# A post-norm attention layer on one core: first keys in float32 from the raw loads, maxima spread through DRAM, and own places for the last unit

## The chip, the core and the metric

The kernel runs on one core of a Trainium2 chip. The core has TensorE (matrix products, in the profile PE, its weight loads PEld), VectorE (DVE), ScalarE (ACT), GpSimd (POOL) and SyncE (SP, which here only issues DMAs). The metric is the device time of one execution in microseconds (us); three runs of the kernel before gave 1235.85 us in the median (1235.78 to 1237.4). A difference is given against that median.

## The reference, cut to what matters

Eight sequences of 1024 tokens, 512 features, 16 heads of 32. The attention is linear: queries and keys go through random features, and the keys' features are summed with the values first.

```python
def feature_map(x, orf):                       # orf: 128 x 32
    proj = x @ orf.T / d_k ** 0.25
    norm = jnp.sum(x * x, -1, keepdims=True) / (2.0 * math.sqrt(d_k))
    return (jnp.exp(proj - norm) + 1e-6) / math.sqrt(m)
q = feature_map(split(x @ Wq.T + bq), orf)
k = feature_map(split(x @ Wk.T + bk), orf)
v = split(x @ Wv.T + bv)
buf = concatenate([einsum('nlm,nld->nmd', k, v), sum(k, 1)[..., None]], -1)
out = einsum('nlm,nmd->nld', q, buf)
attn = merge(out[..., :-1] / out[..., -1:]) @ Wo.T + bo
x = layernorm(x + attn)
x = layernorm(x + x @ (ternary(W) * mean(abs(W))).T)
```

Outputs are float32.

## The kernel before, in words

**Blocks and splits.** The 8192 tokens are worked in 16 blocks of 512, two to a sequence. The products with Wk, Wv, Wq and Wo run in float16: each operand is scaled by a power of two, worked out from its largest magnitude, and split into a high and a low half (`high` on ScalarE, `low` on VectorE); a projection is the sum of three products, high times high, low times high, high times low, twelve instructions of 128x512 for each 128 outputs. In the profile these are k_ps, v_ps, q_ps and o_ps (L353, L366), and xh, xl, wh, wl are the halves.

**The largest magnitude.** `Largest` takes the maximum along each partition on VectorE (amax, then acol, one column of 128). To have the maximum of all partitions in every partition, TensorE turns the column into a row (`turn`, amt, L202), VectorE takes the row's maximum (`across`, arow, L207), and TensorE spreads it with a product with ones (`spread`, ams, L211). `scale` then makes the powers of two on VectorE in six or seven one-column steps. This is done once for each of the four weights and for each of the 16 blocks of x.

**A block's way.** Keys: projection, clamp and split on VectorE and ScalarE, a trip through DRAM that stacks the parts head by head (ds, st; the squared norms go by dn), features (kf_ps, L626), exponentials on ScalarE (e), and the sums over tokens (kvt_ps on TensorE, esum and vsum on GpSimd). After the second block of a sequence `close` finishes the sums (vs_ps, ks_ps, kv_tp, kv) and `out_scale` works out the scale of the attention's output. Queries go the same way (qf_ps, L765) and then meet the sums (num_ps and den, L784); the denominators go through DRAM to be inverted and spread (dd, r, dr, rb), the quotient (num, L852) is split (oh, ol), projected (o_ps), added to the residual y, normalized, turned (x_tp), multiplied by the ternary weight (f_ps), normalized again and stored.

**The order.** Nothing is scheduled by the tool: the class `Order` sorts every step by a written place, in us, and by what it needs. `pe` and `gen` steps are TensorE's; `after` puts a step so much later than a TensorE step ends, `at` puts it at a place. Each engine and SP's DMA queue then work strictly in that order. A unit is one block's stretch: while the keys and values of block t are made, the queries of earlier blocks are applied and still earlier ones finished. `units` holds the first units' places; the later ones are 74 apart. `E` is the place where the last block's unit ends.

**The head.** The raw loads of w_k (SP) and of x's block 0 (ScalarE's queue) come in four pieces each; VectorE takes their maxima, TensorE spreads them, both are split, and the first key projection can begin. w_v, w_q and w_o are loaded into places that other tiles use later (`STAGING`): w_q and w_o both into the tile rb, which w_k occupies first.

**Buffers that the steps touch.** The pool pj has six PSUM buffers for all products but two accumulators; y has five row tiles; xraw, rb and esum have one each.

Of the kernel before, what the change touches and what calls it, by code (L numbers as in the profile page):

```python
# [9 lines left out]
F32 = mybir.dt.float32  # L10
F16 = mybir.dt.float16
AF = mybir.ActivationFunctionType
# [41 lines left out]
STAGING = {"k": "rb", "v": "esum", "q": "rb", "o": "rb"}  # L54
# [4 lines left out]
class Order:  # L59
# [7 lines left out]
    DRAW = 2.5  # L67
# [63 lines left out]
def tile_postln_layer(  # L131
# [49 lines left out]
    class Largest:  # L181
# [33 lines left out]

        def steps(self, place, gap=3.0, needs=()):

            step = order.pe(place, 0.15, self.turn, needs=needs)
            gate = order.after(step, 0.2, self.across)
            return order.pe(place + gap, 0.15, self.spread, needs=[gate])  # L220
# [27 lines left out]
    class W:  # L248
# [6 lines left out]
        def load(self):  # L255
            self.raw = block(STAGING[self.which], f"wraw_{self.which}")
            nc.sync.dma_start(self.raw, self.src.rearrange("(k p) o -> p k o", p=P))

        def measure(self):
            self.largest.whole(self.raw)  # L260
            self.largest.close()
# [13 lines left out]
        def high(self, kt):  # L275
            nc.scalar.activation(self.h[:, kt, :], self.raw[:, kt, :], AF.Copy, scale=wup[:, self.c])

        def low(self, kt):
            c, raw = self.c, self.raw[:, kt, :]
# [13 lines left out]
    class X:  # L293
# [22 lines left out]
        def unscale(self, which):  # L316

            for w in which:
                d = small([P, 1], f"down_{w}_{self.t}", 24)
                nc.vector.tensor_mul(d, xdown[:, self.c], wdn[:, weights[w].c])  # L320
# [52 lines left out]
    ws = {which: W(src, which) for which, src in (("k", wkT), ("v", wvT), ("q", wqT), ("o", woT))}  # L373
    for w in ws.values():
        w.tiles()
    x0, w0 = X(0), ws["k"]
    w0.raw, x0.raw = block(STAGING["k"], "wraw_k"), block("xraw", "xraw_0")
    for kt in range(KT):
        nc.sync.dma_start(w0.raw[:, kt, :], wkT[kt * P : (kt + 1) * P, :])
        nc.scalar.dma_start(x0.raw[:, kt, :], xT[kt * P : (kt + 1) * P, 0:TB])  # L380
        w0.largest.piece(kt, w0.raw[:, kt, :])
        x0.largest.piece(kt, x0.raw[:, kt, :])


    class Bias:


        def __init__(self, src, which):
# [3 lines left out]
            nc.scalar.dma_start(self.b, src)  # L392
# [8 lines left out]
    biases = {"k": bk, "q": bq}  # L401
    bv_sb = ctile([P, D], F32, "bv_sb")
# [76 lines left out]
    class Stacked:  # L479
# [45 lines left out]
        def project(self, i, places):  # L525
            step = gen(places, 0.87, self.proj(i), needs=self.ready)
            w = self.which
            clamp = after(step, {"k": 0.02, "q": 0.02}[w], self.clamp, i)
            high = after(step, {"k": 1.89, "q": 1.13}[w], self.high, i, needs=[clamp])
            rest = after(step, {"k": 5.33, "q": 3.44}[w], self.remainder, i, needs=[high])  # L530
            s1 = after(step, {"k": 8.5, "q": 2.45}[w], self.spill, i, 1, needs=[high])
            low = after(step, {"k": 7.53, "q": 6.16}[w], self.low, i, needs=[rest])
            s0 = after(step, {"k": 11.3, "q": 6.97}[w], self.spill, i, 0, needs=[low, s1])
# [26 lines left out]
        def norms(self, place):  # L560
            w = self.which
            step = pe(place, 1.0, self.norm, needs=self.sq_gates, tiled=True)
            last = after(step, {"k": 4.37, "q": 0.02}[w], self.norm_high)
            last = after(step, {"k": 2.22, "q": 3.06}[w], self.norm_rest, needs=[last])
            last = after(step, {"k": 2.48, "q": 6.0}[w], self.norm_low, needs=[last])
            last = after(step, {"k": 6.55, "q": 3.88}[w], self.norm_store, needs=[last])
# [21 lines left out]
    class KBlock(Stacked):  # L588
# [27 lines left out]
        def values(self, tt, places, sums):  # L616
# [3 lines left out]
            self.sum_gates.append(after(step, 2.64, self.v_sum, tt, sums, needs=[bias, *self.sum_gates[-1:]]))  # L620
# [24 lines left out]
        def feature(self, i, tt, place, sums):  # L645
# [3 lines left out]
            self.sum_gates.append(after(step, 0.02, self.e_sum, i, tt, sums, needs=[exp]))  # L649
# [88 lines left out]
        def close(self, places, sums):  # L738

            step = pe(places[0], 1.0, self.v_total, sums, needs=[*self.sum_gates, self.last_kv])  # L740
            g0 = after(step, 3.32, self.close_kv, sums)
            step = pe(places[1], 1.2, self.k_total, sums, needs=[g0, *self.sum_gates], tiled=True)
            g1 = after(step, 1.64, self.close_sums)
            step = pe(places[2], 0.9, self.turn, 0, needs=[g0])
            g0 = after(step, 0.84, self.keep, 0)
            step = pe(places[2] + 2.87, 0.9, self.turn, 1, needs=[g0, g1])
            kv_ready[self.b] = after(step, 0.72, self.keep, 1)
            at(places[2] + 5.87, self.out_scale, needs=[*self.ready, self.bv_ready])
# [4 lines left out]
    class QBlock(Stacked):  # L753
# [80 lines left out]
        def attend(self, i, place):  # L834
            step = pe(place, 1.9, self.products, i, needs=[kv_ready[self.b], *(self.gates[HPT * i + j] for j in range(HPT))], tiled=True)
            self.num_gates.append(after(step, 1.66, self.numerator, i))
            if i == KT - 1:
                last = after(step, 0.58, self.denominator)
                for delay, fn in (
                    (1.4, self.denominator_store),  # L840
                    (6.99, self.recip_load),
                    (4.48, self.recip),
                    (7.84, self.recip_store),
                ):
                    last = after(step, delay, fn, needs=[last])
                for j in range(HPT):
                    gap = 0.76 if self.t < NBLK - 2 else 0.0
                    last = after(step, 5.61 + gap * j, self.recip_spread, j, needs=[last])
# [15 lines left out]
        def divide(self, i, place):  # L864
            num = at(place, self.quotient, i, needs=[self.num_gates[i], self.spread])
            high = at(place + 0.72, self.out_high, i, needs=[num])
# [25 lines left out]
        def layernorm(self, step, last, tt, name):  # L892

            w = name[0]
            last = after(step, {"a": 1.5, "f": 1.61}[w], self.moments, tt, name, needs=[last])
            last = after(step, {"a": 0.02, "f": 6.55}[w], self.power, name, needs=[last])
            last = after(step, {"a": 4.16, "f": 1.31}[w], self.shift, name, needs=[last])
            last = after(step, {"a": 5.74, "f": 7.76}[w], self.apply, tt, name, needs=[last])
# [291 lines left out]
```

## Time and profile before

| | |
|---|---|
| median of 3 runs | 1235.85 us |
| the profiled execution's own time | 1237.1 us |
| its span | 1235.3 us |
| mean granted TensorE clock | 0.991 |
| TensorE busy | 1187.5 us, 96% |
| VectorE, ScalarE, GpSimd busy | 854.7, 832.3, 525.2 us |
| DMA | 169 MB, 137 GB/s in the mean |
| first product of block 0's keys | 14.64 us |
| last product | 1225.6 us |

A row of a timeline gives the start in us, the length in us, the engine (SPq is SP's DMA queue), the line, the operation, what it writes and reads, shapes and types, how many instructions were merged (a float32 product counts as two), and in brackets the idle time of the engine just before and what ended it. A row of the waits gives who waited for what, the total us, how many times, and the longest.

### The profile page before, as it was taken

How to read it: one execution, taken by the hardware profiler on the slowest of the kernel's cores; microseconds unless marked ns; L12 is line 12 of the kernel's file. 1: busy time of each engine (PE TensorE's matmuls, PEld its weight loads, DVE VectorE, ACT ScalarE, POOL GpSimd, SP SyncE). 2: the span in 40 equal slices, each digit the busy share in tenths (PEclk: the TensorE clock that was granted, in tenths of full speed). 3: DMA queues.
4: the chain of work that ended last, by engine and by line, in shares of the span. 5: the costliest groups of instructions: out<-in, count | busy, mean ns of one | idle time of the engine just before them, and what ended most of it. 6: DMA issues, size and time to landing. Idle time of an engine off the chain costs nothing.

```text
span 1235.3 us, 23801 instructions
## 1 busy us (share of the span) xinstructions
PE 1187.5 (96%) x8724; PEld 572.1 (46%) x8724; DVE 854.7 (69%) x1849; ACT 832.3 (67%) x1377; POOL 525.2 (43%) x485
## 2 busy tenths in 40 slices
PE   5899999999999999999999999999999999999987
PEld 2344454545545454454545445453544545454333
DVE  7775665776857756686766848577674876648387
ACT  3486678666766867668686667867686776756643
POOL 0148062724446153552627334372444515354222
PEclk9899999999999999999999999999999999999989
DMA  4445455363554536444453545546355453536421
GB/s 164 145 136 160 132 138 168 104 181 92 169 143 127 158 102 187 107 156 135 123 169 102 170 133 147 149 111 184 80 170 151 130 152 94 167 92 195 123 71 69
DMA packets 94821, 169.39 MB, mean 137 GB/s; under 512 B 14736, under 2 KB 48624, under 8 KB 92656
## 3 DMA queue, kind: packets, MB, share of 16 engines
q1 hardware_dynamic: 93296, 166.24, 46.8%
q8 instruction: 69, 1.13, 0.4%
q10 hardware_dynamic: 1408, 1.63, 0.4%
q14 instruction: 48, 0.39, 0.1%
HBM read 108.06 MB, written 59.77 MB: 136 GB/s over the span
## 4 chain that ended last, share of the span: by engine, by line
PE 81%; DVE 10%; ACT 2%; issue 1%; DMA 1%; POOL 0%; POOLq 0%; SPq 0%; ACTq 0%
PE o_ps L366 13%; PE v_ps L366 12%; PE q_ps L353 12%; PE k_ps L353 8%; PE f_ps L958 8%; PE num_ps L784 5%; PE kf_ps L626 5%; PE den L784 4%; PE kvt_ps L660 4%; PE qf_ps L765 4%; PE x_tp L935 2%; DVE num L852 1%; PE n_ps_k L541 1%; DVE ol L862 1%; DVE st_f L871 1%; DVE y L966 1%
## 5 line engine op out<-in xcount | busy, mean ns | idle before, releaser
L643 POOL TENSOR_TENSOR esum<-esum,e 128x512 f32<-128x512 f32 x192 | 248.0, 1294 | 136.8 <-ACT e L631 132.1
L631 ACT ACTIVATE e<-kf_ps 128x512 f32<-128x512 f32 x256 | 150.8, 597 | 124.1 <-PE kf_ps L626 112.1
L769 ACT ACTIVATE qf<-qf_ps 128x512 f32<-128x512 f32 x256 | 142.7, 610 | 44.4 <-PE qf_ps L765 44.4
L914 POOL TENSOR_TENSOR y<-y,bo_sb 128x512 f32<-128x512 f32 x64 | 82.8, 1296 | 110.4 <-DMA y<-in_x_dram 53.7
L880 POOL TENSOR_TENSOR rs_a<-ve_a,neg_half 128x1 f32<-128x1 f32 x64 | 35.8, 559 | 217.1 <-DVE ve_a L875 212.5
L626 PEld LDWEIGHTS <-st_k 98*128 98x128 f16 x1024 | 77.1, 97 | 63.5 <-issue 10.5
L626 PE MATMUL kf_ps<-of,st_k 98*128 98x128 f16 x1024 | 98.3, 219 | 2.5 <-DMA st_k<-dn_k 2.2
L602 DVE SCALAR_TENSOR_TENSOR v<-v_ps,down_v,bv_sb 128x512 f32<-128x512 f32 x64 | 47.7, 746 | 69.8 <-PE v_ps L366 69.6
L493 DVE TENSOR_SCALAR q_ps<-q_ps,top_q,bottom_q 128x512 f32<-128x512 f32 x64 | 52.2, 816 | 62.5 <-PE q_ps L353 62.4
L765 PE MATMUL qf_ps<-st_q,of 98*128 98x512 f16 x256 | 89.3, 382 | 2.2 <-ACT qf L769 1.1
L500 ACT ACTIVATE part_q<-q_ps,bq_sb,down_q 128x512 f16<-128x512 f32 x64 | 49.8, 778 | 56.8 <-DVE q_ps L493 51.2
L366 PEld LDWEIGHTS <-oh 128*128 128x128 f16 x512 | 49.3, 98 | 77.7 <-issue 12.7
L923 DVE SCALAR_TENSOR_TENSOR y<-o_ps,odown,y 128x512 f32<-128x512 f32 x64 | 48.0, 750 | 53.2 <-PE o_ps L366 47.2
L353 PEld LDWEIGHTS <-wh_k 128*128 128x128 f16 x512 | 48.9, 100 | 70.9 <-issue 18.6
L614 POOL TENSOR_TENSOR vsum<-vsum,v 128x512 f32<-128x512 f32 x48 | 62.7, 1306 | 37.7 <-DVE v L602 37.7
L880 POOL TENSOR_TENSOR rs_f<-ve_f,neg_half 128x1 f32<-128x1 f32 x64 | 49.3, 770 | 68.3 <-DVE ve_f L875 45.7
L643 POOL TENSOR_TENSOR esum<-e,e 128x512 f32<-128x512 f32 x32 | 41.1, 1285 | 87.1 <-ACT e L631 87.1
L500 ACT ACTIVATE part_k<-k_ps,bk_sb,down_k 128x512 f16<-128x512 f32 x64 | 50.1, 782 | 41.2 <-DVE k_ps L493 19.4
L366 PE MATMUL o_ps<-wh_o,oh 128*128 128x512 f16 x256 | 67.4, 384 | 8.7 <-DVE kv L723 5.2
L857 ACT CAST oh<-num 128x512 f16<-128x512 f32 x64 | 39.3, 616 | 47.2 <-DVE num L852 47.2
L353 PE MATMUL k_ps<-xh,wh_k 128*128 128x512 f16 x256 | 66.5, 384 | 4.1 <-ACT xh L335 4.0
L366 PEld LDWEIGHTS <-xh 128*128 128x128 f16 x512 | 46.3, 98 | 50.5 <-issue 7.9
(211 smaller groups left out, 2744.4 us busy)
## 6 DMA issues: line engine op xcount, KB each, us to landing
ds_k<-part_k SPq DMA_DIRECT2D x128, 128.0 KB
st_k<-ds_k SPq DMA_DIRECT2D x64, 256.0 KB
ds_q<-part_q SPq DMA_DIRECT2D x128, 128.0 KB
st_q<-ds_q SPq DMA_DIRECT2D x64, 256.0 KB
rb<-dr SPq DMA_DIRECT2D x64, 256.0 KB
y<-in_x_dram SPq DMA_DIRECT2D x64, 256.0 KB
out_dram<-y SPq DMA_DIRECT2D x64, 256.0 KB
xraw<-in_xT_dram SPq DMA_DIRECT2D x15, 1024.0 KB
```

The costliest lines, as they stand in the source:

```text
L353: nc.tensor.matmul(ps, a[:, kt, c], b[kt], start=(n == 0), stop=(n == 3 * KT - 1))
L366: nc.tensor.matmul(ps, a[kt][:, c], wt[:, kt, :], start=(n == 0), stop=(n == 3 * KT - 1))
L500: nc.scalar.activation(part[:, 1, :], self.ps[i], AF.Identity, bias=b, scale=down)
L626: nc.tensor.matmul(ps[:, j, :], self.st[i][0:NF, j, c], of, start=True, stop=True)
L631: nc.scalar.activation(e, self.eps[i, tt], AF.Exp, scale=EXP_SCALE)
L643: nc.gpsimd.tensor_tensor(es, before, self.es[i, tt].rearrange("p j m -> p (j m)"), op=ALU.add)
L765: nc.tensor.matmul(self.qps[n], of, self.st[i][0:NF, j, :], start=True, stop=True)
L769: nc.scalar.activation(e, self.qps[n], AF.Exp, scale=EXP_SCALE)
L784: nc.tensor.matmul(to[DK * j : DK * (j + 1), :], kvl[:, n, i * P + DK * j : i * P + DK * (j + 1)], self.qf[i, j], start=first, stop=last, ...
L880: nc.gpsimd.tensor_tensor(self.rs[name], self.ve[name], neg_half, op=ALU.pow)
L914: nc.gpsimd.tensor_tensor(y, y, bo_sb, op=ALU.add)
L958: nc.tensor.matmul(ps, a[:, kt, :], tern.w[:, kt, :], start=(n == 0), stop=(n == 2 * KT - 1))
```

## The change

Four things are changed together.

1. **Block 0's keys** are multiplied in float32 straight from the raw loads: `project_first` issues, for each of the four pieces, two pairs of 128x512 products. They need neither maxima nor halves; their scale (`down_k`) is a constant, and the clamp and all that follows are as before. w_k is still split, later, for the other blocks.
2. **The largest magnitudes** of w_k, w_q, w_o and of x's blocks 1 to 15 no longer go through TensorE: `store` writes the column of 128 to DRAM, `fetch` reads it back as a row into every partition, and `fold` takes the maximum of the row in each. Only x's block 0 and w_v keep the old way (`steps`).
3. **w_q** is loaded in four rows of its own into the y tiles (and so can be loaded from the start), w_o alone follows w_k in rb.
4. **The places**: nearly all written places and delays are new, the units' starts among them; the last unit (`t == NBLK - 1`) and unit `NBLK - 4` have places of their own, `out_scale` stands 22.06 after the closing's third place where it stood 5.87 after it, and `DRAW` is 2.35.

```diff
-STAGING = {"k": "rb", "v": "esum", "q": "rb", "o": "rb"}
+STAGING = {"k": "rb", "v": "esum", "q": "y", "o": "rb"}
...
-    DRAW = 2.5
+    DRAW = 2.35
...
+        def store(self):
+            self.dm = dram.tile([P, 1], F32, tag="dm", name=f"dm_{self.name}", bufs=4)
+            nc.sync.dma_start(self.dm, self.col)
+
+        def fetch(self):
+            self.every = sb.tile([P, P], F32, tag="every", name=f"every_{self.name}", bufs=2)
+            nc.sync.dma_start(self.every, self.dm.rearrange("p o -> o p").to_broadcast([P, P]))
+
+        def fold(self):
+            self.all = small([P, 1], f"aall_{self.name}", 24)
+            nc.vector.tensor_reduce(self.all, self.every, AX.X, ALU.max)
+
+        def passed(self, place, gaps, needs):
+            last = order.at(place + gaps[0], self.store, needs=needs)
+            last = order.at(place + gaps[1], self.fetch, needs=[last])
+            return order.at(place + gaps[2], self.fold, needs=[last])
...
-                nc.vector.tensor_mul(d, xdown[:, self.c], wdn[:, weights[w].c])
+                if self.t == 0 and w == "k":
+                    nc.vector.memset(d, QK_SCALE)
+                else:
+                    nc.vector.tensor_mul(d, xdown[:, self.c], wdn[:, weights[w].c])
...
-        w0.largest.piece(kt, w0.raw[:, kt, :])
         x0.largest.piece(kt, x0.raw[:, kt, :])
...
+        def project_first(self, kt, half):
+            w, xs = weights["k"], self.xs
+            for i in (2 * half, 2 * half + 1):
+                if kt == 0:
+                    self.ps[i] = pj.tile([P, TB], F32, tag="pj", name=f"k_ps_0_{i}")
+                nc.tensor.matmul(
+                    self.ps[i], w.raw[:, kt, i * P : (i + 1) * P], xs.raw[:, kt, :], start=(kt == 0), stop=(kt == KT - 1)
+                )
...
-            at(places[2] + 5.87, self.out_scale, needs=[*self.ready, self.bv_ready])
+            at(places[2] + 22.06, self.out_scale, needs=[*self.ready, self.bv_ready])
...
+    last = at(-1.8, x0.unscale, "k", needs=[at(-4.01, bk.scale)])
     for kt in range(KT):
+        steps = [pe(-14.0 + 3.44 * kt + 1.72 * n, 1.72, blocks[0][0].project_first, kt, n) for n in range(2)]
+    for i in range(KT):
+        blocks[0][0].projected(i, steps[i // 2])
+    last = [at(4.54, w0.measure), at(-10.92, x0.largest.close)]
+    a = 4.54
+    last[0] = w0.largest.passed(a, (4.68, 7.22, 16.47), last[:1])
+    step = x0.largest.steps(-15.41, 1.5, needs=last[1:])
...
-            p = a - 37.99 if t > 1 else a - 21.95
-            load = at(a - 51.46 if t > 1 else a - 30.62, xs.load, needs=blocks[t - 1][0].ready)
+            p = a - 41.4 if t > 1 else a - 25.44
+            load = at(a - 52.46 if t > 1 else a - 49.75, xs.load, needs=blocks[t - 1][0].ready)
             amax = at(p, xs.measure, needs=[load])
-            step = xs.largest.steps(p + 3.33, needs=[amax])
-            scale = after(step, 1.1, xs.scale)
+            step = xs.largest.passed(p, (1.97, 5.04, 10.48), [amax])
+            scale = at(p + 11.0, xs.scale, needs=[step])
...
+        elif t == NBLK - 1:
+            k0, v0, q0 = 0.0, 27.0, 44.77
+            ks, vs, qs = 3.51, 4.14, 4.04
...
-            d = E + (4.78, 56.27, 73.51)[n]
-            f = E + (46.22, 84.99, 100.65)[n]
+            d = E + (6.46, 57.96, 76.19)[n]
+            f = E + (46.06, 86.62, 85.57)[n]
```

## The prediction

> **What bounds the kernel now.** I read the page first (busy shares, the 40 slices, the chain of waits), then the waits of TensorE, then a table of stages, then timelines of the places that the change touches. The page:
>
> ```profile
> PE 1187.5 (96%) x8724; PEld 572.1 (46%) x8724; DVE 854.7 (69%) x1849; ACT 832.3 (67%) x1377; POOL 525.2 (43%) x485
> PE   5899999999999999999999999999999999999987
> PE 81%; DVE 10%; ACT 2%; issue 1%; DMA 1%; POOL 0%; POOLq 0%; SPq 0%; ACTq 0%
> ```
>
> TensorE is busy 96% of the span, full in every slice but the first two and the last two, and it is 81% of the chain. So a TensorE instruction taken out of the middle is worth its own time; elsewhere what counts is which wait ends last. The stages (columns: stretch, then busy us of PE, PEld, DVE, ACT, POOL, granted clock, DMA):
>
> ```profile
> 0.00:51.00 51.00, 33.30 (x124) 13.28 (x125) 37.79 (x95) 20.85 (x31) 2.25 (x14) 0.93 0.49 159
> 51.00:71.00 20.00, 16.91 (x166) 9.06 (x164) 14.77 (x33) 14.22 (x25) 10.80 (x9) 1.00 0.41 117
> 178.60:250.00 71.40, 71.40 (x538) 35.43 (x535) 47.44 (x94) 49.59 (x83) 37.65 (x33) 1.00 0.51 142
> 470.20:616.70 146.50, 145.49 (x1090) 70.95 (x1088) 102.36 (x220) 102.75 (x171) 65.43 (x60) 1.00 0.48 139
> 1170.80:1235.30 64.50, 49.79 (x225) 23.03 (x224) 52.37 (x126) 26.07 (x38) 17.56 (x24) 0.91 0.21 67
> ```
>
> In 470 to 616 (two blocks) TensorE stands 1.0 us of 146.5. It stands 17.7 us of the first 51, 14.7 of the last 64.5, and at batch closings in the middle:
>
> ```profile
> PE amt_wk L202 <- DVE acol_x L198: 9.9, 1, 9.9
> PE o_ps L366 <- DVE kv L723: 5.2, 5, 1.6
> ```
>
> **Part 1: the spread of x's maxima leaves TensorE.** In a steady block the two small float32 products stand like this in TensorE's timeline:
>
> ```profile
> 511.43 0.39 PE L626 MATMUL kf_ps<-of,st_k 98*128 98x128 f16 x4
> 511.75 0.38 PE L202 MATMUL amt_x<-ident,acol_x 128*1 128x128 f32 x2
> 512.06 0.61 PE L366 MATMUL v_ps<-wl_v,xh 128*128 128x512 f16 x2
> 516.84 1.03 PE L353 MATMUL q_ps<-xl,wh_q 128*128 128x512 f16 x4
> 517.80 0.38 PE L211 MATMUL ams_x<-arow_x,ones 1*128 1x1 f32 x2
> 518.11 0.82 PE L366 MATMUL v_ps<-wl_v,xh 128*128 128x512 f16 x3
> ```
>
> The next v_ps starts 0.31 us after amt_x does, and amt_x about 0.09 us later than a float16 product would have (from 511.43: four kf rows of 55 ns end at 511.65). So 0.40 each; ams_x likewise (517.80 to 518.11, and four q rows of 0.216 end at 517.70). 15 blocks x 0.81 = 12.1 us, and w_o's pair, also in the full stretch, 0.8: **-12.9 us**. Nothing refills these slots.
>
> What it adds: 18 stores and 18 fetches on SP's queue, about 0.33 us of issue each (as for r<-dd), and on VectorE a 128x128 maximum for the 1x128 one (0.27 us); DVE had idle time in each stage, so I cost this at nothing, as long as the fold doesn't wait. The trip through DRAM is priced by the nearest rows, the reciprocals' trip:
>
> ```profile
> 507.65 0.34 SPq L813 DMA_DIRECT2D r<-dd x1
> 511.28 0.34 SPq L823 DMA_DIRECT2D dr<-r x1
> 513.99 1.25 SPq L829 DMA_DIRECT2D rb<-dr x3
> ```
>
> rb is issued 2.4 us after dr's issue ended, which is the store's landing. Two hops are 4.8 us plus two issues, about 5.5 us. In the new order the fold stands 8.5 us after the store by the written places (gaps 1.97 and 10.48), with some 3 us of spare. Behind the fetch at the head of SP's queue stand the dd stores of a q block; three loads (0.45, 0.51, 0.26 us in that order of rows) lie between store and fetch, so the queue is held about 1 us, which only delays reciprocals whose quotients run some 10 us later. From below: nothing is gained beyond the 12.9. From above: the fold holds VectorE where it is late; that is the slower rival.
> A page of the Trainium skill speaks against this trade: DMA: Bandwidth & Descriptors, section "Anatomy of one DMA", puts about 2.0 us of fixed cost on any transfer however small. By it the two hops are 4.0 us, by the rows 4.8; both lie inside the 8.5.
>
> **Part 2: batch closings.** `out_scale` moves 16 us later, and the key projection and o_ps change neighbours. Before, at one closing, VectorE works off nine one-column instructions (552.19 to 554.84, 2.65 us, one of them stretched to 1.15) ahead of the quotient that o_ps waits for:
>
> ```profile
> 553.19 1.15 DVE L228 TENSOR_TENSOR pp_o<-pa_o,pb_o 128x1 f32<-128x1 f32 x1
> 554.84 0.69 DVE L852 TENSOR_TENSOR num<-num,rb 128x512 f32<-128x512 f32 x1
> 556.18 1.02 PE L366 MATMUL o_ps<-wh_o,oh 128*128 128x512 f16 x4 [1.01 <-DVE kv L723]
> ```
>
> In the new order the quotient stands ahead of the nine and behind the copy of kv (0.68 us) and without one rest_k (0.75): over 2 us earlier, against a stand of 1.0. What is late next is an evacuation of k_ps, which six PSUM buffers cover. Ends: 0 (another wait takes over) to -5.2 (all five). I take **-4**.
>
> **Part 3: the head.** Before, TensorE waits 9.92 us for the maxima, does block 0's keys from 14.64 to 30.8 (the first 20 products at half speed, 0.43 us), and starts the queries of block 0 at 50.66 and the keys of block 1 at 70.56. After: 48 float16 products (10.4 us at 0.216) go, 16 float32 ones come. Their price isn't in the trace in this shape; x_tp's four transposes stream 512 float32 columns in 0.87 us (rows of 109 ns, two a transpose), the four column-tiled ks_ps in 1.0 as listed. I take 0.87, so 13.9 us, at most 16. They start when the first pieces have landed (DVE's first maximum runs at 4.59) with the clock low: the old products ran at half speed for 7.7 us from 14.64; I take 5, which loses 2.6. The maxima of x and w_v and their small products sit between them (2 us). End at 4.6+13.9+2.6+2.0 = 23, where the old ended at 30.8.
> Values come next, and are not ready: xup waits for w_v's 2.28 us maximum ahead of it on VectorE, and w_v's four halves (0.67 us each on ScalarE) stand behind two blocks of key work (4 x 0.77 us), so values start near 27 and are paced by halves and remainders to about 31, then run dense: done near 42 (51 before). Then block 0's features wait for its norms' store and load (two hops after about 40: 45), and the first queries for w_q's scale, which stands on VectorE behind the last v and the features' seven small steps: 47. From there 2.4 us of paced products, the rest of q (7.8), kf (3.5), kvt (3.8): keys of block 1 near 66.5, with 2 us more work done than before at 70.56. The removed w_k split (4 x 0.71 on ACT, 4 x 0.74 on DVE) comes back beside the queries; x's second block is multiplied at 66 and its transfer starts when the float32 products free xraw (23), so it isn't late. Loss and gain: 0 to -9, and I take **-4**.
> The clock speaks against it. The rows: after the 2.7 us stand at 35.37 the granted clock falls to 0.60 and 0.72 for 35 to 45. The Trainium skill, TensorE: Matmul & The Clock Gate, "HAM oscillation", says that an idle window of some 3.4 us throttles the clock to half; the stand that I foresee at 23 to 27 is of that size. By the row nothing more is lost than my 42 holds (1 to 2 us); by the rule one more window at half speed, 1.7 us, and the head would be -2.
>
> **Part 4: the end.** From 1170.8 on VectorE is the bound: 52.4 of 64.5 us, and 58.9 us pass from its first add (1172.70) to its last (1231.6). Block 15's quotients start at 1191.63 though their reciprocals were stored at 1179.43. In the new order one f tile of block 13 (1.76 us of VectorE) goes ahead of that point, f of 14 is laced into o of 15, and the quotients no longer wait for a fourth add. A dense VectorE would end 7 us earlier; the reciprocal of 15 stands behind more work than before (1.5 us later), and lacing could cost 4. Ends +4 and -7, and I take **-3**.
>
> **Sum.** The profiled execution took 1237.1 (span 1235.3 and 1.8 around it): 1237.1 - 12.9 - 4 - 4 - 3 = 1213.2. It was 1.3 above the median 1235.85, so on the median's footing 1212.
>
> **Rivals.**
> 1. Only TensorE's own time goes: head and end give nothing and half of the closings' stands come back elsewhere. For it: 14.7 us of standing in the end are VectorE's. Against: nothing else is full. 1237.1 - 12.9 - 2.6 - 1.3 = 1220.
> 2. All of it comes: 12.9 + 5.2 + 9 + 7 = 34, so 1202. Against: VectorE would have to be gapless.
> 3. Slower: the folds. Each waits at the head of VectorE's queue for every_x, and k_ps, q_ps and v_ps evacuate behind it; once the six PSUM buffers are full (a projection fills one in 12 x 0.216 = 2.6 us, a feature group in 0.22) TensorE stands. It decides from 24/15 = 1.6 us of lost TensorE time a block; with 2.5 a block the time is 1212 + 37 = 1249. For it: SP's queue waited 128.9 us in all for part_q alone, with single waits of 6.3 us, so a fetch can slip past its 3 us of spare. Against: beyond that slip the buffers still cover a part.
> 4. The float32 products don't shorten the head: w_v and the norms' trip end it at the same time as before (block 1's keys at 70). Then 1216.
>
> **How the numbers follow.** Chances: forecast 0.55 (its own range 1205 to 1219; it takes in rival 4), rival 1 0.22, rival 2 0.11, rival 3 0.08, and 0.04 for losses that about cancel. From 1202, rival 2's end, to 1227, which is rival 1 with the end's upper bound of +4 and 2 to 3 more of new standing, lies over 0.8. A measurement of this kernel tells about 0.2% (2.5 us) from no change. Faster 0.90, same 0.03, slower 0.07.
>
> **What would show it.** Part 1: no amt_x or ams_x from block 1 on, 144.9 us or less from one closing to the next but one where 146.5 was; wrong, if DVE lists waits at aall for DMA. Part 2: no stand before o_ps at closings. Part 3: sixteen k_ps rows from about 4.6 to 23, block 1's keys near 66. Part 4: from the last den to the end about 61 us (64.5). The forecast is wrong if TensorE's gaps in the middle grow past 10 us, or if the first queries come after 50.

## The result, and the profile after

The changed kernel takes 1332.03 us (median of 6 runs, 1328.06 to 1336.39), the kernel before 1235.95 beside it (6 runs, 1235.55 to 1238.11): a ratio of 1.077, with an interval of 1.075 to 1.078. It is 96 us slower, and 1212 was forecast. The profiled execution took 1328.06 us, span 1326.3. One execution of the run tr_after further down took 3136 us, in a slow state, and is left out of that run's median.

The page of the changed kernel, in the order in which it was read before: busy shares, two rows of the 40 slices, the chain.

```profile
PE 1206.2 (91%) x8636; PEld 577.8 (44%) x8636; DVE 889.1 (67%) x1849; ACT 820.3 (62%) x1377; POOL 532.6 (40%) x485
...
PE   7466989899899989989899998999989898999987
...
PEclk9778999999899999999899998999989998999999
...
PE 61%; DMA 20%; DVE 13%; ACT 3%; issue 2%; POOL 1%; SPq 1%; ACTq 0%; POOLq 0%; DVEq 0%
```

TensorE is no longer full in any long stretch, its clock falls in many slices, and DMA, 1% of the chain before, is 20% of it. The waits name the trip of the maxima (columns: us in all, times, longest); first those of all engines:

```profile
DVE aall_x L226 <- DMA every_x<-dm_x: 108.8, 15, 11.9
...
PE kf_ps L679 <- DMA st_k<-dn_k: 34.5, 3, 16.9
...
PE kf_ps L679 <- ACT e L684: 25.0, 12, 4.3
PE v_ps L401 <- DVE xm L214: 24.5, 6, 5.4
```

and those of SP's queue:

```profile
SPq L222 <- DMA dm_x<-acol_x: 84.1, 14, 7.9
```

One block of the steady part, from the timelines of SP's queue, of VectorE and of TensorE:

```profile
560.01 0.35 SPq L218 DMA_DIRECT2D dm_x<-acol_x  x1
...
567.54 0.35 SPq L222 DMA_DIRECT2D every_x<-dm_x  x1
```

```profile
572.21 0.29 DVE L226 TENSOR_REDUCE aall_x<-every_x 128x1 f32<-128x128 f32 x1 [5.50 <-DMA every_x<-dm_x]
```

```profile
569.72 1.03 PE L401 MATMUL v_ps<-wl_v,xh 128*128 128x512 f16 x4
574.94 0.38 PE L679 MATMUL kf_ps<-of,st_k 98*128 98x128 f16 x4 [4.18 <-ACT e L684]
575.16 1.23 PE L401 MATMUL v_ps<-wh_v,xl 128*128 128x512 f16 x4
576.18 1.91 PE L401 MATMUL v_ps<-wh_v,xh 128*128 128x512 f16 x4
```

The store's landing took 7.2 us (560.36 to 567.54) where the prediction had 2.4, and the fetch stood 5.6 us of them at the head of SP's queue (three loads were issued in between). The fold came 12.2 us after the store's issue, where the written order has 8.5. VectorE stood 5.5 us for it, TensorE 4.2 (the features' evacuations on ScalarE stand behind xh, which needs the new scale), and four products after the stand take 1.91 us instead of 1.03. The granted clock says the same (columns as in the tables of stages before):

```profile
561.00:566.00 5.00, 5.00 (x40) 2.75 (x33) 0.99 (x2) 3.93 (x7) 2.99 (x3) 1.00 1.16 81
566.00:571.00 5.00, 4.75 (x33) 2.65 (x32) 0.71 (x2) 0.00 (x0) 2.05 (x2) 1.00 0.18 34
571.00:576.00 5.00, 1.06 (x8) 0.61 (x8) 3.44 (x18) 2.32 (x5) 0.97 (x1) 0.99 0.29 89
576.00:581.00 5.00, 5.00 (x17) 1.95 (x16) 4.96 (x6) 1.45 (x3) 4.92 (x5) 0.67 0.14 48
```

The clock is 0.67 in the five us after the stand. The first row holds a second clue: right after the store the DMA engines are all busy and move 81 GB/s. The trace's records of single packets show it finer. Packets of 4096 bytes (the loads of the stacks) have a median of 0.19 us in both kernels, but 466 of 12288 take over 0.8 us (called slow packets below) in the changed kernel and 30 before, and 442 of the 466 begin within 10 us after the issue of one of the 18 stores of maxima.

Three marks of each trace split the span: the start of the first attention output (o_ps of block 0), the end of the last den, the end of the span.

| | first o_ps | to the last den | to the end | span |
|---|---|---|---|---|
| before | 189.6 | 981.2 | 64.5 | 1235.3 |
| changed | 228.0 | 1040.0 | 58.2 | 1326.3 |
| difference | +38.4 | +58.8 | -6.3 | +91.0 |

### The profile page after: what moved, and what is told of

It reads as the page before. It is cut to its first block, busy times and chain, and to the rows that moved or that the text cites. A ratio compares the mean times of both kernels' runs of the same rounds, so it can differ in the third digit from the quotient of the medians.

```text
span 1326.3 us, 23764 instructions
## 1 busy us (share of the span) xinstructions
PE 1206.2 (91%) x8636; PEld 577.8 (44%) x8636; DVE 889.1 (67%) x1849; ACT 820.3 (62%) x1377; POOL 532.6 (40%) x485
## 4 chain that ended last, share of the span: by engine, by line
PE 61%; DMA 20%; DVE 13%; ACT 3%; issue 2%; POOL 1%; SPq 1%; ACTq 0%; POOLq 0%; DVEq 0%
PE q_ps L388 12%; PE k_ps L388 10%; PE o_ps L401 8%; DMA dm_x<-acol_x 8%; PE f_ps L1011 7%; PE v_ps L401 6%; DMA every_x<-dm_x 4%; PE kvt_ps L713 4%; PE kf_ps L679 3%; DMA dn_k<-n_k 3%; PE qf_ps L818 2%; PE num_ps L837 2%; PE den L837 2%; DVE amax_x L194 2%; DVE y L976 1%
## 5 line engine op out<-in xcount | busy, mean ns | idle before, releaser
L696 POOL TENSOR_TENSOR esum<-esum,e 128x512 f32<-128x512 f32 x192 | 260.1, 1359 | 174.8 <-ACT e L684 167.7
L684 ACT ACTIVATE e<-kf_ps 128x512 f32<-128x512 f32 x256 | 144.8, 599 | 97.2 <-PE kf_ps L679 67.8
L822 ACT ACTIVATE qf<-qf_ps 128x512 f32<-128x512 f32 x256 | 145.7, 616 | 33.5 <-PE qf_ps L818 27.5
L370 ACT ACTIVATE xh<-xraw,xup 128x512 f16<-128x512 f32 x64 | 45.8, 726 | 113.7 <-DVE xup L253 113.7
L401 PE MATMUL v_ps<-wh_v,xh 128*128 128x512 f16 x256 | 76.3, 425 | 27.4 <-DVE xm L214 24.5
L401 PEld LDWEIGHTS <-xh 128*128 128x128 f16 x512 | 50.8, 104 | 83.0 <-issue 45.9
L933 POOL TENSOR_TENSOR rs_f<-ve_f,neg_half 128x1 f32<-128x1 f32 x64 | 43.6, 682 | 94.6 <-DVE ve_f L928 47.9
L226 DVE TENSOR_REDUCE aall_x<-every_x 128x1 f32<-128x128 f32 x15 | 4.3, 286 | 108.8 <-DMA every_x<-dm_x 108.8
L943 ACT ACTIVATE y<-y,mr_a,rs_a 128x512 f32<-128x512 f32 x64 | 53.3, 833 | 37.4 <-DVE mr_a L937 37.4
L943 ACT ACTIVATE y<-y,mr_f,rs_f 128x512 f32<-128x512 f32 x64 | 51.9, 813 | 37.9 <-DVE mr_f L937 37.2
```

Source lines behind the costliest of these rows:

```text
L401: nc.tensor.matmul(ps, a[kt][:, c], wt[:, kt, :], start=(n == 0), stop=(n == 3 * KT - 1))
L684: nc.scalar.activation(e, self.eps[i, tt], AF.Exp, scale=EXP_SCALE)
L696: nc.gpsimd.tensor_tensor(es, before, self.es[i, tt].rearrange("p j m -> p (j m)"), op=ALU.add)
L822: nc.scalar.activation(e, self.qps[n], AF.Exp, scale=EXP_SCALE)
L933: nc.gpsimd.tensor_tensor(self.rs[name], self.ve[name], neg_half, op=ALU.pow)
L943: nc.scalar.activation(y, y, AF.Identity, bias=self.ve[name], scale=self.rs[name])
```

## The experiments

Times are medians; each ratio is to the kernel before on the same chip, whose medians were 1236.8 to 1238.9. "Pace" is the stretch from the third attention output to the thirteenth, ten blocks: 731.8 us before, 778.6 in the changed kernel. Where a part of it is given to a tile, it is the time from the start of each of that tile's products to the start of the next instruction on TensorE.

**Which part loses the time.** Run xte:

```diff
-            step = xs.largest.passed(p, (1.97, 5.04, 10.48), [amax])
-            scale = at(p + 11.0, xs.scale, needs=[step])
+            step = xs.largest.steps(p + 3.33, needs=[amax])
+            scale = after(step, 1.1, xs.scale)
...
```

> The changed kernel with the largest magnitudes of the x blocks 1 to 15 spread again by the two small products on TensorE, at the places that the kernel before had relative to the measure (turn at p + 3.33, scale 1.1 after the second product); the three weights still go by way of DRAM. Theory A (the trip of x's maxima is late in every block, VectorE stands at its fold and TensorE loses 5 to 6 us a block by it): the stands of 3 to 5 us once a block go, two blocks take 145 to 147 us where the changed kernel takes 157, and the time is about 1236 + 18.7 (the later start of block 1's keys stays) - 5.5 (the shorter end) - 4 (the closings) = 1245, between 1238 and 1255. Rival B (the new places of the steady blocks lose the time, whoever spreads the maxima): two blocks stay above 152 us and the time above 1300.

1258.6 us, ratio 1.015 (1.014 to 1.017). The stands of 3 to 5 us in the steady blocks are gone (none over 1.4 us is left from block 3 to the last den) and the pace is 734.7. B is out. A has the stands right, but the time lies above its range (1245 expected, at most 1255).

Run allte, in addition:

```diff
-            step = w.largest.passed(a, (0.16, 7.52, 7.65), needs)
-            scale = at(a + 16.86, w.scale, needs=[step])
+            step = w.largest.steps(a + 2.84, 2.13, needs=needs)
+            scale = after(step, 2.13, w.scale)
```

and w_k in the same way.

> As the run xte, and the maxima of w_k, w_q and w_o go by the two small products too, so that nothing of the trip through DRAM is left: what remains of the change are the float32 keys of block 0 and the places. Theory A: the stand of 16.9 us ahead of block 0's features goes with the trip of w_k, block 1's keys start near 67 to 72 where they start at 89 in the changed kernel, and the time is 1222 (1214 to 1232). Rival C (the float32 keys themselves make the head longer): block 1's keys start later than 78 and the time is above 1233.

1248.3 us, ratio 1.007 (1.005 to 1.009). The first o_ps came at 202.5 where it is 212.6 in xte, but 13 us later than before, and block 1's keys start at 79.9 (70.6 before), so the head stays long without any trip. C has the numbers, but the float32 products themselves ran as quickly as forecast (see Part 3 below): TensorE stood 5.2 us for the features' set-up on VectorE, and 3.5 and 2.8 us for the rows of the small products, whose places were chosen for this run.

Run xtrip, in the kernel before:

```diff
-            step = xs.largest.steps(p + 3.33, needs=[amax])
-            scale = after(step, 1.1, xs.scale)
+            step = xs.largest.passed(p, (1.97, 5.04, 10.48), [amax])
+            scale = at(p + 11.0, xs.scale, needs=[step])
...
```

> The kernel before with one part of the change alone: the maxima of the x blocks 1 to 15 go by way of DRAM with the changed kernel's gaps (store 1.97, fetch 5.04, fold 10.48, scale 11.0 after the measure's place); all else is the kernel before. Theory A: VectorE stands at the fold in every block and the time is 1236 + 15 x 5 = 1311 (1280 to 1330). Rival B (the loss is of the new places): two blocks take 145 to 147 us and the time is 1222 to 1236.

1333.0 us, ratio 1.074 (1.071 to 1.078): x's trip alone costs as much as the whole change, and a little more than A's 1280 to 1330. But not as A said. VectorE stands only 19 us in all at folds; it stands 102.6 us for r<-dd, the reciprocals' load, which before costs it 18.7. One place in SP's queue and on VectorE, then the waits of VectorE and of SP's queue:

```profile
551.31 0.34 SPq L218 DMA_DIRECT2D dm_x<-acol_x  x1
551.75 1.27 SPq L826 DMA_DIRECT2D dd<-rd  x4
559.14 0.34 SPq L222 DMA_DIRECT2D every_x<-dm_x  x1
...
561.14 0.34 SPq L831 DMA_DIRECT2D r<-dd  x1
```

```profile
565.06 0.55 DVE L835 RECIPROCAL r<-r 128x64 f32<-128x64 f32 x1 [8.89 <-DMA r<-dd]
```

```profile
DVE r L835 <- DMA r<-dd: 102.6, 14, 10.0
```

```profile
SPq L222 <- DMA dm_x<-acol_x: 83.6, 15, 7.0
```

The load itself is hardly slower (3.7 us from its issue to the reciprocal in the mean, 3.0 before). It is issued late, 6.5 to 9.4 us after the last dd store in twelve blocks, 2.0 to 2.8 us before: the fetch stands ahead of it at the head of SP's queue until the store has landed. Few loads follow the store at once here, and only 103 packets are slow.

Run early:

```diff
+            sooner = 8.0 if t > 1 else 0.0
-            load = at(a - 52.46 if t > 1 else a - 49.75, xs.load, needs=blocks[t - 1][0].ready)
-            amax = at(p, xs.measure, needs=[load])
-            step = xs.largest.passed(p, (1.97, 5.04, 10.48), [amax])
+            load = at(a - 52.46 - sooner if t > 1 else a - 49.75, xs.load, needs=blocks[t - 1][0].ready)
+            amax = at(p - sooner, xs.measure, needs=[load])
+            step = xs.largest.passed(p, (1.97 - sooner, 4.0, 10.48), [amax])
```

> The changed kernel with the load, the measure and the store of x's maxima 8 us sooner for the blocks 2 to 15, the fetch 1 us sooner, and the fold, the scale and the rest where they were: 18.5 us from measure to fold in the written order where there were 10.5. Theory A (only the room for the trip was too small; store and fetch take 12 us from issue to fold where the order gave 8.5): no wait of VectorE at the fold over 1 us, two blocks at about 145 us, and 1332 - 14 x 5.9 = 1249 (1240 to 1262). Rival D (the store itself holds up the other transfers of SP's queue and the loads of the stacks come late by it, whenever it is issued): the stands remain, only the wait changes its name, and the time stays above 1290.

1271.0 us, ratio 1.024 (1.021 to 1.027), pace 738.4. Between A and D: more room takes most of the stands away, but VectorE still waits 42 us at folds, TensorE 15 us between 300 and 1150 for stacks whose norm loads came late, and 195 packets are slow.

**What the store itself does.** Four runs of the kernel before with one store more per block that nothing reads; first run d4:

```diff
+        def spare(self):
+            dm = dram.tile([P, 1], F32, tag="dm", name=f"dm_{self.name}", bufs=4)
+            nc.sync.dma_start(dm, self.col)
...
+            at(p + 2.6, xs.largest.spare, needs=[amax])
```

> The kernel before, with one store more in each of the blocks 1 to 15: the column of x's 128 maxima, 128 pieces of 4 bytes, goes to a DRAM tile that nothing reads, at p + 2.6 on SP's queue. Nobody waits for it. Theory D (such a store slows the transfers around it: in the changed kernel 466 packets of 4096 bytes took over 0.8 us, in the kernel before 30, and they lie in the 6 us after each store): over 150 such packets, loads of the stacks that land some us later, and 1240 to 1270. Rival E (the store costs only those who wait for it; the slow packets belong to the fetch, or to the order of the loads): at most 60 such packets and 1236 to 1241.

1307.6 us, ratio 1.056 (1.055 to 1.058). That is above the 1240 to 1270 of theory D. A store of 512 bytes for which nobody waits costs 70 us in 15 blocks; 519 packets are slow. One place, SP's queue and VectorE, and the stretch after the store:

```profile
537.07 0.35 SPq L218 DMA_DIRECT2D dm_x<-acol_x  x1
...
539.18 0.34 SPq L817 DMA_DIRECT2D r<-dd  x1
550.14 0.34 SPq L827 DMA_DIRECT2D dr<-r  x1
```

```profile
549.27 0.55 DVE L821 RECIPROCAL r<-r 128x64 f32<-128x64 f32 x1 [9.14 <-DMA r<-dd]
```

```profile
537.50:547.50 10.00, 8.18 (x55) 4.40 (x54) 1.35 (x2) 3.94 (x7) 7.52 (x7) 1.00 0.88 30
```

For 10 us the DMA engines are 88% busy and move 30 GB/s. Nearly all of that time is of 4096-byte packets, the stacks' loads (135 of 138 us, summed over the 16 engines); no packet of 4 bytes in it is recorded with more than 9 ns. So the trace shows the loads held up, and not the store's own pieces at work. The load r<-dd, issued behind the store, lands 9.8 us after its issue ended, and VectorE stands for it with v's evacuations behind.

Run d4far: `dram.tile([P, P], ...)` and `nc.sync.dma_start(dm[:, 0:1], self.col)`.

> As the run d4, but the 128 pieces of 4 bytes go 512 bytes apart in DRAM instead of next to each other. If it is writing many pieces into the same 512 bytes that slows the others, there are at most 60 packets of 4096 bytes over 0.8 us and the time is 1236 to 1241; if small pieces do it wherever they go, the packets and the time are those of d4.

1238.6 us, ratio 1.0009 (0.9998 to 1.0020); 13 slow packets. The same place in SP's queue:

```profile
506.86 0.35 SPq L218 DMA_DIRECT2D dm_x<-acol_x  x1
...
508.88 0.34 SPq L817 DMA_DIRECT2D r<-dd  x1
512.57 0.34 SPq L827 DMA_DIRECT2D dr<-r  x1
```

As many pieces of the same size on the same queue cost nothing that can be told from noise when they do not lie together. From r<-dd to dr it is 3.7 us; in d4 it is 11.0.

Run d4by64: `dram.tile([P, 16], ...)`, so 64 bytes from one piece to the next.

> As the run d4far, with the 128 unread pieces of 4 bytes 64 bytes apart in DRAM instead of 512. If the pieces hinder one another within 64 bytes, nothing is lost: 1236 to 1241. If within 512 bytes, 8 pieces meet where 128 did, and the time lies between 1240 and 1260.

1240.1 us, ratio 1.0015 (1.0002 to 1.0028); 15 slow packets. So nearly all of the cost (5.6%) comes only where the pieces lie closer than that; 64 bytes apart they cost at most 0.3%.

Run d512: `dram.tile([P, P], ...)` and `nc.sync.dma_start(dm, ident)`.

> As the run d4, but the unread store writes 128 pieces of 512 bytes (the constant identity, 64 KB) instead of 128 pieces of 4 bytes: the same place and number of pieces. If small pieces are what slows the others, there are at most 60 packets of 4096 bytes over 0.8 us and the time is 1236 to 1241; if any store at this place does it, they are as many as in d4 or more.

1237.9 us, ratio 1.0007 (0.9993 to 1.0021); 21 slow packets. 64 KB in pieces of 512 bytes cost at most 0.2% here, 512 bytes in pieces of 4, side by side, cost 70 us.

**The places without the trip.** Run mix: the kernel before, with the changed delays, `close`, `divide`, and the places of the blocks from 3 on and of the end.

> The kernel before with its own head (keys of block 0 in float16, its places for the blocks 0 to 2) and its small products on TensorE for all maxima, at the places from p = a - 37.99 on, but the changed kernel's places for the closings, the steady blocks from block 3 on, and the last unit. It tells what those places are worth by themselves. By the runs xte and allte the closings' stands give 5 us over ten blocks (the gap of TensorE after the keys, 110.1 to 104.1) and the end 5 us: 1226 (1218 to 1236). If the gain at the closings comes back as standing elsewhere, 1232 to 1242.

1254.2 us, ratio 1.013 (1.011 to 1.015): a miss. The end is 58.4 us as forecast and k_ps gives its 5.8 us, but the pace is 746.0: 9.1 us more after q_ps, 4.5 after qf_ps, 3.5 after n_ps_q. The changed places were written for a TensorE without the small products; which of these products' neighbours costs what was not followed.

**Mending the store.** The column is put into a tile of 128x32 that is zero elsewhere, turned on VectorE in squares of 32, and four rows of 128 bytes are stored:

```diff
-            self.col = small([P, 1], f"acol_{self.name}", 24)
-            nc.vector.tensor_reduce(self.col, self.parts, AX.X, ALU.max)
...
+            wide = wides[int(self.name[1:]) % 2]
+            nc.vector.tensor_reduce(wide[:, 0:1], self.parts, AX.X, ALU.max)
+            self.laid = small([P, 32], f"laid_{self.name}", 4)
+            nc.vector.transpose(self.laid, wide)
...
-            nc.sync.dma_start(self.dm, self.col)
+            nc.sync.dma_start(self.dm.rearrange("(b j) o -> b (j o)", j=32), self.laid.rearrange("(b j) c -> b j c", j=32)[:, 0, :])
```

Run tr_after, for x in the changed kernel:

> The changed kernel, with the store of x's maxima as 4 pieces of 128 bytes in place of 128 pieces of 4 bytes, for the blocks 1 to 15: the column is turned in squares of 32 by 32 on VectorE (one instruction more) and four rows of 32 maxima are stored. The places, the fetch, the fold and the 8.5 us between store and fold are as in the changed kernel; the weights' trips too. Theory F (the 128 pieces of 4 bytes in one stretch of 512 bytes are what made store and neighbours late): store and fetch land in about 2.4 us each, VectorE's waits at the fold sum to under 10 us (108.8), under 60 packets of 4096 bytes over 0.8 us (466), and the time is 1236 + 20 (longer head, with the weights' trips) - 19 - 5 = 1232 (1222 to 1245). Rival A (the room of 8.5 us was too small for any trip past the loads of SP's queue): the waits at the fold stay above 50 us and the time above 1280.

1242.3 us, ratio 1.004 (1.003 to 1.006): 90 us come back with the places as they were. Its profile is from a second run:

> The run tr_after once more, for its profile: two blocks in 143.9 us where the changed kernel takes 157 and the kernel before 146.5; VectorE's waits at the folds of x under 30 us in all; no stand of TensorE over 1.4 us after block 2.

1244.5 us. Pace 721.2, 9 slow packets, VectorE's waits at x's folds 27.7 us, no stand over 1.4 us from block 3 on until the end. Theory F holds, though the waits at the folds stay above the 10 us that it expected first; and A's "too small for any trip" falls: the same 8.5 us do for a store that lands. The DRAM tile is the same column of 128 as in the changed kernel, so it is the form of the store and not the tile's place that counts.

Run tr_xtrip, the same store in xtrip:

> The run xtrip (the kernel before with x's maxima through DRAM, nothing else changed) with the store as 4 pieces of 128 bytes. Theory F: 1236 - 15 x 0.81 = 1224 (1218 to 1236), where xtrip took 1333. Rival A: above 1290.

1252.6 us, ratio 1.013 (1.010 to 1.016). Of xtrip's 94 us 80 are gone, but the gain of 12 is a miss: kvt_ps takes 8.7 us more in ten blocks, where TensorE waits for ScalarE's evacuations of the features. A late scale is not the reason: it comes 11.4 us after the start of the values of the block before in the mean of ten blocks, by the small products 16.0. What of the order costs this was not followed. 74 packets are slow, the longest 1.6 us, where in xtrip the longest of 103 took 7.1; the reciprocals' load costs VectorE 38.4 us (102.6 in xtrip, 18.7 before).

Run tr_mix:

> The kernel before with its own head and its small products for the weights and the blocks 0 and 1, the changed kernel's places for closings, steady blocks and end, and x's maxima of the blocks 2 to 15 through DRAM with the store as 4 pieces of 128 bytes. Theory F and the pace of the changed kernel without its stands (719 us for ten blocks, the kernel before 731.8): 1236 - 19 - 5 = 1212 (1205 to 1222). If the standing of TensorE ahead of the features (1.0 us every second block in the run mix) stays, 1215 to 1225.

1228.2 us, ratio 0.992 (0.991 to 0.994): faster than both kernels, pace 718.9 as said, but above the 1205 to 1222 expected. The first o_ps came at 199.5, ten us later than before. TensorE's timeline has a reason for some of it; first the run mix, then tr_mix:

```profile
52.37 0.38 PE L202 MATMUL amt_x<-ident,acol_x 128*1 128x128 f32 x2 [1.48 <-DVE acol_x L198]
52.68 1.04 PE L353 MATMUL q_ps<-xl,wh_q 128*128 128x512 f16 x4
```

```profile
53.56 0.59 PE L211 MATMUL amt_x<-ident,acol_x 128*1 128x128 f32 x2 [3.04 <-DVE acol_x L202]
54.08 1.89 PE L384 MATMUL q_ps<-xl,wh_q 128*128 128x512 f16 x4
```

A stand of 1.48 us costs 1.48; one of 3.04 also halves the clock for what follows, up to 59.9. Run tr_mix2 places that product later:

```diff
-                step = xs.largest.steps(p + 3.33, needs=[amax])
+                step = xs.largest.steps(p + (3.33 if t > 1 else 5.5), needs=[amax])
```

and leaves block 2's maxima on TensorE too.

> As the run tr_mix, with block 2's maxima on TensorE as in the kernel before, and block 1's turn 2.2 us later, so that TensorE does not stand 3.0 us for block 1's column at 53.6 (after which its products ran at half speed to 59.5). If that stand and the clock after it made the head of tr_mix longer, the first attention output starts at 193 to 195 where tr_mix has 200, and the time is 1221 to 1225; if block 2 or the stand is shifted elsewhere, 1226 to 1230.

1222.0 us, ratio 0.987 (0.986 to 0.989), first o_ps at 195.7 (193 to 195 expected): 15 us less than the kernel before beside it (1237.3), and the fastest version here. At the same place it still stands, for almost as long, but the products after it run at full speed:

```profile
54.26 0.38 PE L659 MATMUL kf_ps<-of,st_k 98*128 98x128 f16 x4 [2.98 <-DMA st_k<-dn_k]
...
54.88 1.04 PE L384 MATMUL q_ps<-xh,wh_q 128*128 128x512 f16 x4
```

So what went is the lowered clock and not the stand. The two edits were not tried apart.

**All of the change, with the store mended.** Run tr_all: w_q, w_k and w_o also store four rows.

> As the run tr_after, and the stores of the maxima of w_q, w_k and w_o too are 4 pieces of 128 bytes: nothing of the change is left out but the form of the store. Theory G (the head is longer by its order: VectorE has the maxima of three weights, block 0's keys and the features' set-up ahead of the first features, and TensorE's stands of 3 us and more halve its clock for what follows): the first attention output of block 0 starts at 200 to 206, where the kernel before has 190 and the run allte 202, and the time is 1230 to 1238. Rival H (the longer head was the weights' stores of 4-byte pieces): it starts at 192 or sooner and the time is 1220 to 1228.

1227.2 us, ratio 0.992 (0.990 to 0.994): 105 us less than the changed kernel, and faster than the kernel before, by the form of a store alone. Its page, the waits, and two blocks beside the same stretch of the changed kernel:

```profile
PE 1177.3 (96%) x8636; PEld 568.1 (46%) x8636; DVE 901.6 (74%) x1867; ACT 821.7 (67%) x1377; POOL 534.9 (44%) x490
...
PE   7778999999999999999999999999999999999987
```

```profile
DVE aall_x L235 <- DMA every_x<-dm_x: 23.4, 7, 4.7
```

```profile
485.00:629.00 144.00, 144.00 (x1082) 70.46 (x1081) 108.66 (x223) 101.26 (x172) 67.32 (x60) 1.00 0.51 143
```

```profile
539.20:696.20 157.00, 148.56 (x1082) 71.76 (x1081) 107.45 (x221) 100.77 (x171) 66.42 (x60) 0.97 0.53 131
```

The first of the two tables is tr_all, the second the changed kernel, both with 1082 instructions of TensorE. The 13.0 us between them are 8.4 of standing (157.00 - 148.56) and 4.6 of products at a lowered clock (148.56 - 144.00). From store issue to fold the mean of 15 blocks is 6.4 us in tr_all and 12.0 in the changed kernel; from the end of the store's issue to the issue of the fetch, which waits for its landing, it is 2.1 and 7.8. In tr_all SP stood only 5.0 us in all for it, so 2.1 is a bound from above.
Of the head, tr_all leaves +8.4 (first o_ps 198.0): the time is H's, the mark lies between G's and H's, and each had a part. The weights' three stores made 16.1 of the changed kernel's 38.4 (tr_after_b, 214.1, to tr_all), x's stores of the first blocks 13.9 (228.0 to 214.1), and 8.4 are left with the store mended.

## Why the prediction was wrong, by its own steps

**Part 1, the gain: right.** Without amt_x and ams_x, and with the 1.9 us less after q_ps that is their neighbours' delay, ten blocks of tr_all are 8.1 us shorter than before: 0.81 a block, as worked out.

**Part 1, the trip: here the forecast failed.** The step was "rb is issued 2.4 us after dr's issue ended, which is the store's landing", used as the price of a hop, and from it "some 3 us of spare" and "the queue is held about 1 us". The landing took 7.8 us on average, the queue was held 6.0 (84.1 us in 14 waits), and the spare was negative. The row was the nearest by queue and number of pieces, but dr writes 128 pieces of 256 bytes, dm 128 pieces of 4 bytes side by side. d4, d4far, d4by64 and d512 show that this is what counts. By run early this late landing is the larger part in the changed kernel: 8 us more of room give back 40 of the 59 us that the mended store of tr_all gives back in the pace (778.6, 738.4, 719.4). The bounds missed a second cost: not what a hop takes, but what the store does to other transfers; d4 pays 70 us with no hop to wait for. The mended store, at most 2.1 us, lands as the step had assumed.
The 2.0 us that the prediction takes from the Trainium skill, DMA: Bandwidth & Descriptors, "Anatomy of one DMA", stand there for transfers issued by GpSimd; these are issued by SP.
The Trainium skill, DMA: Bandwidth & Descriptors, "Specifications", says that below 512 bytes DMA does a read-modify-write; the prediction passed over it. It points the right way, and the runs limit it: pieces of 4 bytes that lie 64 bytes apart, also below that size, cost at most 0.3% here. That 16 writes into one stretch of 64 bytes must follow one another would fit 10 us for 128 pieces (about 0.08 us each, an estimate from d4's window), but is argued and not shown: the records of single packets do not show the pieces taking that time.

**Part 2, closings: right.** In tr_all no stand of 1 us ahead of o_ps is left in the middle, and the time after k_ps falls by about 5.4 us over the five closings in ten blocks (110.1 to 104.6). Taken were 4, with 5.2 as the most, for the whole run.

**Part 3, the head: wrong in sign.** -4 was taken, with 0 to -9; with the store mended it is +8.4 (tr_all). The early steps held: the float32 products ended at 23.5 (23 forecast; 0.93 to 1.00 us each at full clock, not 0.87), values ran from 26.3 to 40, and the first features came at 47.8 in tr_all (45). What failed is "From there 2.4 us of paced products, the rest of q (7.8), kf (3.5), kvt (3.8): keys of block 1 near 66.5". They start at 74.9 in tr_all and 89.2 in the changed kernel, 70.6 before. TensorE does not run dense there; tr_all's timeline:

```profile
47.83 1.03 PE L688 MATMUL kf_ps<-of,st_k 98*128 98x128 f16 x8 [7.11 <-DMA st_k<-dn_k]
48.66 2.17 PE L397 MATMUL q_ps<-xh,wh_q 128*128 128x512 f16 x4
...
70.72 1.15 PE L688 MATMUL kf_ps<-of,st_k 98*128 98x128 f16 x16 [3.81 <-DMA st_k<-ds_k]
74.89 1.87 PE L397 MATMUL k_ps<-xh,wh_k 128*128 128x512 f16 x4 [3.02 <-ACT e L693]
```

The last stack of block 0 was issued at 61.97, behind the queries' spills and w_o's load on SP's queue, which the prediction did not walk through. And the stand ahead of the features, 4 us by the forecast's own numbers (values done at 40 to 42, features at 45), was not charged with its clock: it was 7.1 us, and the four products after it took 2.17 us. The rule that spoke against the step, with -2 instead of -4, leaned the right way. Of the +8.4, 4.3 are there when block 1's keys start; the rest comes in the unit after it, 50.2 us from block 1's keys to block 2's where it was 45.3. In tr_mix, with the old head, it is 50.4, so that rest does not need the float32 keys; what makes it was not followed.

**Part 4, the end: right in sign, undersized.** From the last den to the end it is 57.1 to 58.6 us in every kernel with the new places, 64.5 before: -6.1 for -3, near the -7 of a dense VectorE.

**The sum, with the store mended:** head +8.4, middle -13.6, end -6.1, so -11.3 in the span, where the forecast had -4, -16.9 (parts 1 and 2) and -3, so -23.9. The store's form then adds 102.3: 30.0 in the head, 72.4 from there to the last den, -0.2 in the end.

**Rival 3** described what the profile shows, VectorE standing at the fold, and "a fetch can slip past its 3 us of spare" was the right doubt. Its price of 2.5 us a block was less than half of the 5.9 that the pace shows (778.6 - 719.4 over ten blocks). In the two blocks set beside tr_all's above it was 4.2 of standing and 2.3 of the lowered clock for each, and the clock was not in the price. And the fold is only where the wait shows in this order: xtrip loses 94 us with 19 us of waiting there, and the queue held for the same landing. Its chance of 0.08 rested on the row for dr as well.
On the clock: in the changed kernel's steady blocks stands of TensorE of 2.79 and 2.90 us were followed by no products at the lowered clock, and the ten of 3.6 us or more by 5 to 10 such products each. The 3.4 us of the Trainium skill, TensorE: Matmul & The Clock Gate, "HAM oscillation", lie between. The bound is not sharp: 3.04 us were enough in tr_mix where 2.98 in tr_mix2 were not, and 2.7 us were in the head of the kernel before (the stand at 35.37 of the prediction).

## What to carry to other kernels

Price a small store by its pieces and by where they land, not by its bytes or by another store's latency: neighbouring pieces of 4 bytes can hold up the transfers behind them, and an unread copy of the store, put into the old kernel, measures that in one run. When waits grow in several places that share only a DMA queue, look for what was issued just before them; a high busy share of the DMA engines with few GB/s was the sign here. And charge a TensorE stand of 3 us and more about half as much again for the clock after it; here it was 4.6 us for 8.4 of standing.

## What the runs showed of the hardware

A store of 128 pieces of 4 bytes into 512 adjacent bytes of DRAM left the DMA engines 88% busy at 30 GB/s for 10 us, nearly all of it loads held up (run d4), made 519 of 12288 packets of 4096 bytes slower than 0.8 us (30 in the kernel before, 13 with the pieces 512 bytes apart, 15 with 64), and cost 70 us in 15 blocks with no reader. The way round it is cheap:

```profile
L207 DVE STREAM_TRANSPOSE laid_x<-wide x15: 211/211/213, 56.4 to 1009.0; 128x32 f32<-128x32 f32 x15
```

0.21 us of VectorE lay a column of 128 values as four rows of 128 bytes, and their store landed in at most 2.1 us in the mean.
